# Four places in the order of a decoder layer on one core: a silu that no longer empties the list of deferred parts, the expert choice a step behind its logits, attention's reciprocal in three links of a step each, and the gate behind the next step's input

## The chip, the cores and the metric

The kernel runs on one core of one Trainium2 chip, as one program. The metric is the device time of one execution in microseconds (us), as the median of several runs. Engines are called by their short names: PE (TensorE; PEld is its loading of weights), DVE (VectorE), ACT (ScalarE), POOL (GpSimd) and SP (SyncE, here only a queue that issues DMAs).

## What is computed

One decoder layer on x of shape 8 x 512 x 512 (B x S x D), all in fp32:

```python
x = _layernorm(x + _L0_attn_ref(x, ...))           # a Mamba block
x = _layernorm(x + _L0_xattn_ref(x, ctx, ctx, mask, ...))  # cross attention, 16 heads of 32
x = _layernorm(x + _L0_ffn_ref(x, ...))            # 32 experts, 4 of them for each token

def scan_fn(h, inp):                               # in the Mamba block, over the sequence
    dA_t, dBx_t, C_t = inp
    h = dA_t * h + dBx_t
    y_t = jnp.einsum('bdn,bn->bd', h, C_t)
    return (h, y_t)
...
y = y * jax.nn.silu(z)                             # the gate
...
attn = jax.nn.softmax(scores, axis=-1)             # attention; the row sums are divided out
...
_, gtop = jax.lax.top_k(group_scores, LG)          # the choice: 4 of 8 groups of experts, then 4 experts
_, idx = jax.lax.top_k(masked, K)
...
z = jax.nn.silu(xf @ sw1) * (xf @ sw3) @ sw2       # a shared expert, for all tokens
```

The Mamba block has an inner width of 1024 and 16 states for each channel, so the recurrence runs over 8 x 1024 x 16 sequences of 512 steps. An expert takes at most 640 tokens; which place a token gets there is counted in token order.

## The kernel before

The program has three parts: `layers` (Mamba, attention, choice, shared expert), `experts` and `finish` (the last layernorm). The change lies in `layers`.

`layers` walks over 16 chunks of 256 tokens, two for each of the 8 batches; in the profile the even chunk of a pair is the first half of a batch. A chunk has 32 steps: 4 quarters q of the channels, 4 groups g of states, and 2 halves ci. A step's own work is on DVE: `steps_in` (L489, dtx times B, into the tile h), `scan` (L496, the recurrence as one scan instruction along 4 x 257 elements) and `collect` (L503, h times C). ACT computes the decays exp(A dt) of the following step ahead (`decays`, L477, four instructions); `carry` (L483, ACT) hands the state over. The sums over the states are matmuls (`products`, L513 and L523) into the PSUM tile py, issued one step later. B and C come as the tiles bc by DMAs from SP (L418), six tiles in rotation. After each 8 steps a quarter's py is complete: `gated` (L537, DVE) multiplies it into zs, and this also frees py, of which there is one. The next quarter's first product (L513) therefore stands behind the gate. `gated` runs at the beginning of the steps with k % 8 == 1.

Around this core all other work is laid in as parts: the next chunk's input (layernorm, flips, convolution, `prepare` for dt and dtx), the chunk's z (`gate_x`) and its silu at step 8, the silu of the next chunk's xs at step 24, the output projection of the chunk before (`back`, L554 and L563), and the parts of `units(b - 1)`: the whole attention, choice and shared expert of the batch before, spread by weights over the two chunks. So batch 0's Mamba has no such parts beside it, chunks 2 to 15 have those of batches 0 to 6, and the last batch's parts come after the loop, with no scan beside them.

The order on ACT, DVE and PE is the order in which this Python emits instructions (`manual_schedule`); SP's and POOL's order is a scheduler's. A part emits its PE work and returns its rest as a function, which goes into the list `left`. Each step is cut into thirds, `run(0)` ahead of the scan, `run(1)` behind the decays and `run(2)` behind `collect`; each of them calls `settle`, which runs what is due in the list. A plain function is due at the next third, one given by `wait(part)` three thirds, so one step, later. `dry()` runs all of the list at once, whatever its due time:

```python
def wait(part):
    return (clock[0] + 3 if clock else 0), part
...
def dry(force=True):
    while settle(force):
        pass
```

`finish_silu` (steps 8 and 24) calls `dry()` and then `silu` (L393 and L394: it loads ACT's table for silu, applies it, and loads the table of ln and exp again).

The parts of `units` that matter here, in their order:

- Attention, for each of 8 pairs of heads i: `maximum` (PE L831, DVE L833), `negate` (PE L840, ACT L844, DMAs L847), `weigh` (PE L857, ACT L861), `gather` (PE L873), and after its fourth piece `split` (ACT L885 copies po to raw; four DMAs, L893 and L894, bring raw to attT and to total). After each second pair, so for each of four head groups oc, `divide(oc)`: on ACT Ln and Exp(-x) of total into r (L902 and L903), on DVE a Newton step (`newton`, L906 to L908), which also multiplies attT. Since Ln and Exp are emitted in `divide` itself, Newton is due a third later.
- `output` (PE L768, DVE L925 and L926) and a layernorm, for 4 row blocks; `flip2` (PE L938, ACT L939).
- `hidden("sw1")` (PE L768, ACT L956), and after its first block `pick` (PE L590, the logits in the PSUM tile ps_l), which returns `choose` (DVE L597 to L626). From there a chain with `wait` ahead of each link: `best` four times (L633 to L642), `weights` (L648 to L657), `place` (PE L676 and L677 into the PSUM tile ps_b), `locate` (DVE L682 to L695) and 16 sends of rows to the experts' slots (L706, POOL). In chunks 3 to 13 the odd chunk's `finish_silu` at step 24 finds this chain in the list.
- `hidden("sw3")` (PE L768, DVE L954), the silu of the hidden layer, `shared` (PE L768, DVE L975 into z).

Buffers that tie these parts together: raw, nm, r, z and some others share one tag "row" with two buffers; total has one; the PSUM tag "mm" of two buffers holds ps_l, ps_b, ps_m, po and the ps_p of all dense products.

Of the kernel before, what the change touches and what calls it, by code (L numbers as in the profile page):

```python
# [8 lines left out]
F32 = mybir.dt.float32  # L9
I32 = mybir.dt.int32  # L10
U8 = mybir.dt.uint8
AF = mybir.ActivationFunctionType
ALU = mybir.AluOpType
# [4 lines left out]
P = 128  # L18
B, S, D = 8, 512, 512
DC = D // P  # L20
# [66 lines left out]
def layers(ctx, tc, a, x1d, filld, based, xbuf):  # L87
# [23 lines left out]
    nc = tc.nc  # L111
# [8 lines left out]
    p3 = ctx.enter_context(tc.tile_pool(name="l_p3", bufs=2))  # L120
# [162 lines left out]
    left, clock = [], []  # L283

    def wait(part):

        return (clock[0] + 3 if clock else 0), part
# [5 lines left out]
    def settle(force=False):  # L293

        due, later = [], []
        for x in left:
            (due if force or not clock or x[0] <= clock[0] else later).append(x)
        for _, part in due:
            rest = part()
            if rest:  # L300
                later.append(rest if isinstance(rest, tuple) else (0, rest))
        left[:] = later
        return due
# [4 lines that stand above are left out]
# [82 lines left out]
    def silu(*tiles):  # L390

        for v in tiles:
            tc.keep_in_program_order(nc.scalar.activation(v, v, AF.Silu))  # L393
        tc.keep_in_program_order(nc.scalar.preload_act_table_set(LN_EXP))  # L394
# [16 lines left out]
    def bcast(f, g):  # L411

        got = []
        for r0 in (g * NG, NST + g * NG):
            t = bcp.tile([P, NG // 2, T], F32, tag="bc", name="bc")
            for r in range(2):
                n0 = r0 + r * NG // 2
                nc.sync.dma_start(  # L418
                    t[r * HP : (r + 1) * HP], f["scr"][n0 : n0 + NG // 2, :].partition_broadcast(HP)
                )  # L420
            got.append(t.unsqueeze(1).to_broadcast([P, 2, NG // 2, T]))
        return got
# [63 lines left out]
    def steps_in(c, h, dtx, bc):  # L486

        steps = h.rearrange("p (j m) t -> p j m t", j=2)[:, :, :, 1:]
        nc.vector.tensor_tensor(  # L489
            steps, dtx[:, c % 2].unsqueeze(2).to_broadcast([P, 2, NG // 2, T]), bc[0], ALU.mult  # L490
        )
# [41 lines left out]
    def gated(q, f):  # L533

        f["xs"].pop(q)
        pair = f["zs"][:, 2 * q : 2 * q + 2, :]
        nc.vector.tensor_tensor(pair, pair, f["py"], ALU.mult)  # L537
# [46 lines left out]
    def pick(b, x2t, x2T, st):  # L584


        pl = psm.tile([P, SC, E], F32, tag="mm", name="ps_l")
        for j in range(SC):
            for dc in range(DC):
                nc.tensor.matmul(  # L590
                    pl[:, j, :], x2T[:, dc, j * P : (j + 1) * P], wg[:, dc, :], start=(dc == 0), stop=(dc == DC - 1)
                )
        return lambda: choose(b, x2t, pl, st)

    def choose(b, x2t, pl, st):
        m1 = new([1], "g_m1")
# [174 lines left out]
    def units(b):  # L771

        st = {}
# [124 lines left out]
        def divide(oc):  # L898

            attT, total = st["attT"], st["total"]  # L900
            r = p3.tile([P, D], F32, tag="row", name="r")
            nc.scalar.activation(r, total, AF.Ln)  # L902
            nc.scalar.activation(r, r, AF.Exp, scale=-1.0)  # L903

            def newton():
                nc.vector.tensor_tensor(total, total, r, ALU.mult)  # L906
                nc.vector.scalar_tensor_tensor(total, total, -2.0, r, ALU.add, ALU.mult)
                nc.vector.scalar_tensor_tensor(  # L908
                    attT[:, oc, :], attT[:, oc, :], -1.0, total, ALU.mult, ALU.mult
                )  # L910

            return newton

        def output(lt):
            if lt == 0:
# [76 lines left out]
        late = []  # L992
# [72 lines left out]
    def do(fn, *args, first=False):  # L1065

        if first:
            dry(False)
        rest = fn(*args)
        settle()  # L1070
        if rest:
            left.append(rest if isinstance(rest, tuple) else (0, rest))

    def finish_silu(*tiles):
        dry()
        silu(*tiles)

    def work(k):

        front = 6.9 if k in (2, 3) else 3.4 if 4 <= k < 8 or k in (14, 16, 19, 22, 25) else 1.0 if k in (13, 27) else 0.0  # L1080
        return 1.2 + front

    f = {"xt": x0}
# [13 lines left out]
    bc, n = bcast(f, 0), 0  # L1097
# [7 lines left out]
    for i, (b, t) in enumerate(chunks):  # L1105
        nf = {}
        after = chunks[i + 1] if i + 1 < len(chunks) else None
        if t == 0:
            side, spent = units(b - 1) if b else sources(0), 0.0

            own = [work(k) for k in range(len(steps))] * 2
            whole = sum(own) + sum(x[0] for x in side)
        for k, (q, g, ci) in enumerate(steps):
            if ci == 0:
                if (q, g) != (CC // 2 - 1, NST // NG - 1):
                    bcn = bcast(f, (g + 1) % (NST // NG))
                else:
                    bcn = bcast(nf, 0) if after else None
            h = ahead

            parts = []

            def part(fn, *args, first=False):
                parts.append((do, fn, *args, first))

            if k in (2, 3) and old:
                part(back, k - 2, *old)
            if 4 <= k < 8:
                part(gate_x, k - 4, f)
            if k == 8:  # L1130
                parts.append((finish_silu, f["zs"]))
            if k % 8 == 3:
                if q + 1 < CC // 2:
                    part(prepare, q + 1, f)
                elif after:
                    part(prepare, 0, nf)
            if after:
                if k == 10:
                    part(norm_x, nf)
                if k == 13:  # L1140
                    for j in range(DC // 2):
                        part(flip_x, j, nf)
                if k in (14, 16, 19, 22):
                    part(convolve, after[1], (14, 16, 19, 22).index(k), nf, first=(k == 14))
                if k == 24:
                    parts.append((finish_silu, *nf["xs"].values()))
                if k == 25:
                    part(x_proj, nf)
            if side and (k >= 4 or t and k < 2):
                at = t * len(steps) + k + 1  # L1150
                while side and spent + sum(own[:at]) <= whole * at / len(own):
                    w, fn, alone = side.pop(0)
                    spent += w
                    part(fn, first=alone)
            thirds = [[], [], []]
            for m, x in enumerate(parts):
                thirds[round((m + 0.5) * 3 / len(parts) - 0.5) if x[0] is do else 1].append(x)

            def run(m):
                clock[0] += 1  # L1160
                settle()
                for x in thirds[m]:
                    if x[0] is do:
                        do(*x[1:-1], first=x[-1])
                    else:
                        x[0](*x[1:])

            if k % 8 == 1:
                if k > 1:
                    gated(q - 1, f)  # L1170
                elif old:
                    gated(CC // 2 - 1, old[2])
            steps_in(2 * q + ci, h, f["ready", q][1], bc)
            if i == 0 and k == 0:
                load("Wo")
            if i == 0 and k == 2:
                biases()
            if k == 0 and old:
                twice_x(*old)
            if k == 7 and after:  # L1180
                load_x(*after, nf)
            run(0)
            scan(t, 2 * q + ci, g, das[n % 2], h)
            n += 1

            if k + 1 < len(steps) or after:
                nq, ng, ni = steps[(k + 1) % len(steps)]
                ahead = carry(t if k + 1 < len(steps) else after[1], 2 * nq + ni, ng)
                decays(2 * nq + ni, ng, (f if k + 1 < len(steps) else nf)["ready", nq][0], das[n % 2])
            run(1)  # L1190

            if products:
                products()
            products = collect(2 * q + ci, g, h, bc, f)
            run(2)
            if ci == 1:
                bc = bcn
            while i < 2 and cleared < E * (i * len(steps) + k - 6) // (2 * len(steps) - 7):
                clear(cleared)
                cleared += 1  # L1200
        while t and side:
            _, fn, alone = side.pop(0)
            do(fn, first=alone)
        old = (b, t, f)
        f = nf
# [357 lines left out]
```

## Time and profile before

| | |
|---|---|
| median of 3 runs | 5744.45 us (5741.9 to 5746.47) |
| the profiled execution | 5746.82 us, its span 5745.1 us |
| mean granted PE clock | 0.92 |
| first scan begins, last scan ends | 58.3 us, 3882.1 us |
| batch of chunks 6 and 7 | 1446 to 1937 us: PE 405.79, DVE 438.78, ACT 255.85 us busy of 491 |
| scan L496 | 512 x 2297 ns |
| L503, L489 | 512 x 1223 ns, 512 x 1218 ns |
| gate L537 | 64 x 681 ns |
| Newton L906, one of its three instructions | 32 x 692 ns |
| L902, L903 | 32 x 619 ns, 32 x 629 ns |
| table load in silu | 1283 ns, two for each silu |

A line of the groups or of a timeline names the engine, the line of the kernel, the operation and the tiles it writes and reads, then its shapes, and, where the engine stood idle before it, how long and what ended that. A line of the waits names the waiting engine, line and tile, then, after the arrow, the engine, line and tile that released it, then the total in us, the number of times, and the longest.

### The profile page before, as it was taken

The numbers are of one execution on the slowest core, as the hardware profiler recorded it, in microseconds if no ns is written. First come the engines' busy times: TensorE is split into PE (matmuls) and PEld (weight loads), VectorE is DVE, ScalarE is ACT, GpSimd is POOL, SyncE is SP. The second block draws the span as 40 slices with busy tenths as digits, with TensorE's granted clock in tenths as the row PEclk, the third lists the DMA queues.
The fourth block names the chain that finished last, engine by engine and source line by source line (L and its number), as shares of the span: only waits on it lengthen the run. The fifth ranks groups of instructions, "written<-read, shape, count | busy, mean of one in ns | idle before, by whom it ended". The sixth has DMA issues, their size and how long they took to land. (4 is left out here: it accounts for less than half of the span.)

```text
span 5745.1 us, 60272 instructions
## 1 busy us (share of the span) xinstructions
PE 4856.4 (85%) x19752; PEld 2720.4 (47%) x19752; DVE 4463.2 (78%) x5738; ACT 2507.0 (44%) x5428; POOL 485.5 (8%) x424
## 2 busy tenths in 40 slices
PE   5668878887887888788698878878899999999995
PEld 3334334433433433343343434333477777777773
DVE  6898988998898898889889888984355555555554
ACT  4454554564455455446455545632222222222223
POOL 0000001001000100100010010000111111111111
PEclk7879989998998999899899989989899999999997
DMA  6677355444534534453363444333245455444444
GB/s 190 208 220 214 100 135 156 123 117 130 168 98 117 175 112 123 138 157 111 91 202 94 133 142 142 108 95 119 78 113 123 123 123 123 123 123 123 123 122 146
DMA packets 554282, 769.83 MB, mean 134 GB/s; under 512 B 135754, under 2 KB 268394, under 8 KB 551920
## 3 DMA queue, kind: packets, MB, share of 16 engines
q1 hardware_dynamic: 517952, 677.55, 40.5%
q0 software_dynamic: 33280, 76.90, 7.2%
q10 hardware_dynamic: 2736, 11.54, 0.5%
q8 instruction: 156, 2.56, 0.2%
q14 instruction: 158, 1.29, 0.1%
HBM read 508.68 MB, written 165.05 MB: 117 GB/s over the span
## 5 line engine op out<-in xcount | busy, mean ns | idle before, releaser
L496 DVE TENSOR_TENSOR_SCAN h<-l_da,h 128x1028 f32<-128x1028 f32 x512 | 1176.0, 2297 | 67.8 <-ACT l_da L477 37.2
L477 ACT ACTIVATE l_da<-both,l_aneg 128x256 f32<-128x256 f32 x2048 | 872.6, 499 | 402.4 <-DVE h L496 396.9
L523 PE MATMUL py<-h,l_twice 128*64 128x256 f32 x4096 | 601.0, 415 | 133.8 <-DVE h L503 133.8
L503 DVE TENSOR_TENSOR h<-h,bc 128x1024 f32<-128x1024 f32 x512 | 626.1, 1223 | 12.5 <-DVE l_state L498 0.3
L489 DVE TENSOR_TENSOR h<-both,bc 128x1024 f32<-128x1024 f32 x512 | 623.4, 1218 | 6.5 <-DMA bc<-scr 6.4
L523 PEld LDWEIGHTS py<-h,l_twice 128*64 128x64 f32 x4096 | 285.8, 145 | 444.9 <-DVE h L503 180.1
L1312 PE MATMUL ps_h<-xT,w 128*128 128x320 f32 x1536 | 435.5, 433 | 0.0
L861 ACT ACTIVATE eT<-ps_t 128x1024 f32<-128x1024 f32 x256 | 260.1, 1019 | 274.2 <-PE ps_t L857 274.1
L833 DVE TENSOR_REDUCE mx<-ps_s 128x2 f32<-128x1024 f32 x256 | 310.9, 1218 | 83.9 <-PE ps_s L831 79.5
L1392 POOL DMA_INDIRECT based<-y,xe x160 | 253.2, 1582 | 1312.1 <-ACT y L1415 574.1
L831 PE MATMUL ps_s<-l_ka,l_qa 64*128 64x512 f32 x1024 | 313.2, 688 | 54.8 <-DVE mx L833 53.0
L873 PE MATMUL po<-eT,l_va 128*64 128x512 f32 x1024 | 285.2, 631 | 87.1 <-ACT eT L861 43.4
L1333 DVE TENSOR_TENSOR hT<-ps_h,p 128x320 f32<-128x320 f32 x128 | 63.0, 492 | 378.6 <-PE ps_h L1312 378.6
L1312 PEld LDWEIGHTS ps_h<-xT,w 128*128 128x128 f32 x1536 | 292.2, 190 | 118.2 <-issue 0.4
L857 PE MATMUL ps_t<-l_qa,l_ka 64*128 64x512 f32 x1024 | 279.7, 617 | 40.6 <-DVE mx L833 35.0
L1312 PE MATMUL ps_h<-t,s 128*128 128x320 f32 x1024 | 286.1, 432 | 0.0
L768 PE MATMUL ps_p<-x2T,wa 128*128 128x512 f32 x512 | 262.9, 665 | 6.6 <-ACT x2T L939 4.7
L342 PE MATMUL ps_x<-xnT,wm 128*128 128x256 f32 x1024 | 250.5, 401 | 0.3 <-ACT xnT L331 0.3
L342 PE MATMUL ps_z<-xnT,wm 128*128 128x256 f32 x1024 | 241.1, 389 | 6.3 <-DMA wm<-in_in_proj_w 6.3
L554 PE MATMUL po<-wm,zs 128*128 128x512 f32 x512 | 234.3, 611 | 10.8 <-DVE k L753 7.6
L1312 PEld LDWEIGHTS ps_h<-t,s 128*128 128x128 f32 x1024 | 194.6, 190 | 81.1
L342 PEld LDWEIGHTS ps_x<-xnT,wm 128*128 128x128 f32 x1024 | 202.7, 202 | 62.5 <-issue 23.9
(231 smaller groups left out, 7342.3 us busy)
## 6 DMA issues: line engine op xcount, KB each, us to landing
bc<-scr SPq DMA_DIRECT2D x1024, 128.0 KB
w<-in_w SPq DMA_DIRECT2D x93, 1024.0 KB
wm<-in_in_proj_w SPq DMA_DIRECT2D x128, 512.0 KB
xbuf<-zero SPq DMA_DIRECT2D x32, 1362.5 KB
xe<-xbuf SPq DMA_DIRECT2D x32, 1362.5 KB
both<-dt SPq DMA_DIRECT2D x256, 128.0 KB
both<-dtx SPq DMA_DIRECT2D x256, 128.0 KB
wm<-in_out_proj_w SPq DMA_DIRECT2D x64, 512.0 KB
```

What stands on the lines that cost most here:

```text
L342: nc.tensor.matmul(ps[:, i, :], w[:, dc, i * P : (i + 1) * P], f["xnT"][:, dc, :], start=(dc == 0), stop=(dc == DC - 1),)
L477: nc.scalar.activation(da[:, n, 1:], dt[:, c % 2, j, :], AF.Exp, scale=aneg[:, c, j, g, m : m + 1])
L489: nc.vector.tensor_tensor(steps, dtx[:, c % 2].unsqueeze(2).to_broadcast([P, 2, NG // 2, T]), bc[0], ALU.mult)
L496: nc.vector.tensor_tensor_scan(flat, da.rearrange("p n t -> p (n t)"), flat, 0.0, ALU.mult, ALU.add)
L503: nc.vector.tensor_tensor(steps, steps, bc[1], ALU.mult)
L523: nc.tensor.matmul(py[j * HP : (j + 1) * HP, c % 2, :], twice, h[:, j * 2 + m, 1:], start=False, stop=(s == (NST // NG - 1, NG // 2 - 1, 1)),)
L768: nc.tensor.matmul(ps, lhs(dc), rhs(dc), start=(dc == 0), stop=(dc == DC - 1))
L831: nc.tensor.matmul(ps[:, j, :], qa[r, lt * P : (lt + 1) * P], ka[r, :], start=True, stop=True)
L833: return lambda: nc.vector.tensor_reduce(mx[:, lt, :].unsqueeze(2), ps, AX.X, ALU.max) and None
L857: nc.tensor.matmul(ps[:, j, :], ka[r, kc * P : (kc + 1) * P], qa[r, :], start=True, stop=True)
L873: nc.tensor.matmul(po[j * 2 * HD : (j + 1) * 2 * HD, :], va[:, kc, i, j * HD : (j + 2) * HD], eT[:, j, :], start=(kc == 0), stop=(kc == SC ...
L1312: nc.tensor.matmul(ps, w[:, n, r * P : (r + 1) * P], x[:, n, :], start=not more and n == 0, stop=n == 1, skip_group_check=more,)
```

## The change

Nothing is computed in another way; four things are emitted at other places.

1. `pick` returns `wait(choose)`: the choice is due a step after its logits were issued, not at the next third.
2. In `divide`, for the head groups 0 to 2, Ln and Exp are emitted a step later, and Newton a step after them. The last group has no waits.
3. `finish_silu` empties the list only if `clock` is empty, that is outside the loop. In the loop it goes straight to the silu.
4. The gate is emitted behind `steps_in` of its step, not ahead of it.

```diff
--- before.py
+++ after.py
@@ -590,7 +590,7 @@
                 nc.tensor.matmul(
                     pl[:, j, :], x2T[:, dc, j * P : (j + 1) * P], wg[:, dc, :], start=(dc == 0), stop=(dc == DC - 1)
                 )
-        return lambda: choose(b, x2t, pl, st)
+        return wait(lambda: choose(b, x2t, pl, st))
 
     def choose(b, x2t, pl, st):
         m1 = new([1], "g_m1")
@@ -898,18 +898,24 @@
         def divide(oc):
 
             attT, total = st["attT"], st["total"]
-            r = p3.tile([P, D], F32, tag="row", name="r")
-            nc.scalar.activation(r, total, AF.Ln)
-            nc.scalar.activation(r, r, AF.Exp, scale=-1.0)
-
-            def newton():
-                nc.vector.tensor_tensor(total, total, r, ALU.mult)
-                nc.vector.scalar_tensor_tensor(total, total, -2.0, r, ALU.add, ALU.mult)
-                nc.vector.scalar_tensor_tensor(
-                    attT[:, oc, :], attT[:, oc, :], -1.0, total, ALU.mult, ALU.mult
-                )
-
-            return newton
+
+            late = wait if oc < DC - 1 else lambda part: part
+
+            def inverse():
+                r = p3.tile([P, D], F32, tag="row", name="r")
+                nc.scalar.activation(r, total, AF.Ln)
+                nc.scalar.activation(r, r, AF.Exp, scale=-1.0)
+
+                def newton():
+                    nc.vector.tensor_tensor(total, total, r, ALU.mult)
+                    nc.vector.scalar_tensor_tensor(total, total, -2.0, r, ALU.add, ALU.mult)
+                    nc.vector.scalar_tensor_tensor(
+                        attT[:, oc, :], attT[:, oc, :], -1.0, total, ALU.mult, ALU.mult
+                    )
+
+                return late(newton)
+
+            return late(inverse)
 
         def output(lt):
             if lt == 0:
@@ -1072,7 +1078,8 @@
             left.append(rest if isinstance(rest, tuple) else (0, rest))
 
     def finish_silu(*tiles):
-        dry()
+        if not clock:
+            dry()
         silu(*tiles)
 
     def work(k):
@@ -1165,12 +1172,12 @@
                     else:
                         x[0](*x[1:])
 
+            steps_in(2 * q + ci, h, f["ready", q][1], bc)
             if k % 8 == 1:
                 if k > 1:
                     gated(q - 1, f)
                 elif old:
                     gated(CC // 2 - 1, old[2])
-            steps_in(2 * q + ci, h, f["ready", q][1], bc)
             if i == 0 and k == 0:
                 load("Wo")
             if i == 0 and k == 2:
```

## The prediction

> **What bounds the kernel now.** I read the page's busy shares and slices first, then the waits by engine, then, stretch by stretch, the timeline of one batch (chunks 6 and 7, 1446 to 1937 us), whose gaps return in every batch from chunk 2 on.
>
> ```profile
> PE 4856.4 (85%) x19752; PEld 2720.4 (47%) x19752; DVE 4463.2 (78%) x5738; ACT 2507.0 (44%) x5428; POOL 485.5 (8%) x424
> PE   5668878887887888788698878878899999999995
> DVE  6898988998898898889889888984355555555554
> ```
>
> PE leads over the span, but only through the last third (the experts). In the scan loop (first scan 58.3, last ends 3882.1 us) DVE leads:
>
> ```profile
> 1446.00:1937.00 491.00, 405.79 (x1684) 194.32 (x1684) 438.78 (x498) 255.85 (x556) 29.93 (x29) 0.92 0.46 132
> 1868.00:1886.00 18.00, 1.00 (x8) 0.57 (x5) 16.58 (x36) 6.57 (x10) 0.00 (x0) 0.64 0.09 30
> ```
>
> The third number is PE's busy time, the sixth (438.78) DVE's: of 491 us a batch DVE idles 52 and PE 85. PE's idleness is in a few stretches, of which 1868 to 1886 is the emptiest. Elsewhere PE runs without a gap for 25 to 55 us and sets the pace. So the loop is DVE's, with places where DVE stands behind a PE that is solid; 7 batches have the side work.
>
> What DVE waits for:
>
> ```profile
> DVE total L906 <- ACT r L903: 79.7, 16, 12.1
> DVE g_m L597 <- PE ps_l L590: 68.6, 8, 12.4
> DVE h L496 <- ACT l_da L477: 37.2, 21, 9.4
> DVE zs L537 <- ACT zs L393: 25.0, 8, 4.6
> DVE hT L954 <- PE ps_p L768: 18.1, 9, 2.7
> DVE zs L537 <- PE py L523: 8.9, 11, 1.6
> PE ps_b L676 <- DVE g_any L655: 104.2, 7, 17.0
> ```
>
> Columns: total us, times, longest. L906, L597 and L537 are the heads of the parts that the diff moves; the last row is PE waiting for the choice.
>
> [...] L597 stands in DVE's order ahead of L503 and L489 of the next step, and both follow it at 1859.75 and 1860.88 though their scan and their bc had been there during the 8.32 us wait. [...] Here each L393 and L394 load is 1283 ns, 40 times each; the change leaves their number and their places on ACT as they are, so they enter no sum. [...]
>
> **The change part by part.** Removed and added: nothing; instructions per engine stay equal, only places in the orders move. After the loop the orders on PE, ACT and DVE are unchanged, and the experts (4134 us to the end) are the same. So all of it is gaps of the loop.
>
> *The choice a step later.* Before, it stands right behind a scan:
>
> ```profile
> 1843.83 2.29 DVE L496 TENSOR_TENSOR_SCAN h<-l_da,h 128x1028 f32<-128x1028 f32 x1
> 1854.44 0.29 DVE L597 TENSOR_REDUCE g_m<-ps_l 128x4 f32<-128x128 f32 x1 [8.32 <-PE ps_l L590]
> ...
> 1859.75 1.22 DVE L503 TENSOR_TENSOR h<-h,bc 128x1024 f32<-128x1024 f32 x1
> 1860.88 1.22 DVE L489 TENSOR_TENSOR h<-both,bc 128x1024 f32<-128x1024 f32 x1
> 1862.13 2.30 DVE L496 TENSOR_TENSOR_SCAN h<-l_da,h 128x1028 f32<-128x1028 f32 x1
> ```
>
> In the changed order it stands behind L503 and L489, still ahead of the next scan. ps_l doesn't come earlier: PE works without a gap from 1845.17 (shared expert 5.74, ps_l 3.65). So of 8.32 us only L503 + L489 less an overlap of issue, 1.22 + 1.22 - 0.09 = 2.35, is filled; 6.0 stays. 7 x 2.35 = 16.5 us. From both sides: 0 if PE's ps_l slips as much, 7 x 8.3 = 58 if more work came before it, which the order excludes.
>
> *The silu that drains the list.* In odd chunks, at step 24, the deferred choice chain (two rounds of best, weights, placing) was forced out at once. PE's ps_b for it stood ahead of shared-expert matmuls, so PE stood 17.00 us for L655, and then DVE waited for PE: L682 0.73, the gate's py 0.9, L954 1.87, and 0.46 at the scan, 3.5 to 3.96 in chunks 3 to 13. In the changed order the rounds lie in steps 23 to 26, weights in 27, placing in 29, and ps_b comes 46 PE instructions later. The DVE work (best 1.8 each, weights 2.3, placing 5.2 us) is only moved. New: placing holds one of two "mm" PSUM buffers until L684, and the shared z product on PE queues behind that, 0.15 to 0.3 us by L682 + L684 (0.21 x 4 + 0.28 less overlap); ACT's hT, the sends on POOL (16 x 1.3 us) and DVE's later steps are behind it. Net 3.0 x 6 = 18 us; bounds 0 (PE, filled again, is only late elsewhere) and 6 x 4 = 24. At step 8 the order doesn't change, so the 2.91 us wait for silu(zs) in even chunks isn't touched by this edit.
>
> *The reciprocal in three links.* For three of the four head groups Ln and Exp go a step later on ACT, and the Newton step (3 x 0.69 us) another on DVE. Groups 0 and 1 have no gap at L906: 0. The fourth is written without waits and keeps its order. Group 2 has, at step 12 of odd chunks, the first line below:
>
> ```profile
> 1770.37 0.69 DVE L906 TENSOR_TENSOR total<-total,r 128x512 f32<-128x512 f32 x1 [2.74 <-ACT r L903]
> ...
> 1788.36 1.22 DVE L503 TENSOR_TENSOR h<-h,bc 128x1024 f32<-128x1024 f32 x1
> 1789.60 1.31 SPq L418 DMA_DIRECT2D bc<-scr  x2
> 1791.01 0.55 SPq L893 DMA_DIRECT2D attT<-raw  x1
> 1796.49 0.69 DVE L906 TENSOR_TENSOR total<-total,r 128x512 f32<-128x512 f32 x1 [6.92 <-ACT r L903]
> ```
>
> The 2.74 us goes. Whether it is given back is asked of group 3, 20 us on, where DVE waits 6.92 + 1.03 for that group's reciprocal. Its row sums leave PE and ACT by 1785.7 (raw, L885), but SP's queue holds the DMA behind a bc load that waits for DVE's L503, done at 1789.58. So up to 3.9 us of DVE's lead shortens that chain too, and 2.74 fits. I take 2.4 of it (part may end at PE, solid until 1788.3), 6 times, and 1.6 for chunk 15, where the same wait is 2.6 us: 16 us. Bounds: 0, and 7 x 2.7 plus the 6.4 us of chunk 15's last group, 25.
> The added waits: the total<-raw DMAs of the next group (total has one buffer) now wait for L907/L908 of the group before, on SP, with bc loads behind them. For group 3 they would issue from 1778.8 on, and Newton, 2.07 us behind the scan that begins about 1773.7, ends at 1778.1: covered, by 0.7 us; if not, a bc load 3 steps ahead of its use is late by less than that lead. r holds one of two "row" buffers longer, so in group 0 ACT's nm (L844) waits some 5 us for the Newton step with four decays (1.70 us) behind it; replayed with the durations above, these are ready 3 us before their scan. 0; without that cover about 2 to 5 us a batch, and this goes into the range.
>
> *The gate behind steps_in.* At step 1 of each 8, DVE does L489 (1.22) before the gate (0.68). Where the gate waits, for zs (25.0 us, 8 times) or py (8.9, 11 times), up to 1.2 us of L489 goes into the wait: at most 8 x 1.2 + 7.6 = 17, some 10 inside the periodic stretches. Against it, PE gets its next py buffer 1.22 us later, 64 times. Where PE is solid behind a gate (1450.4 to 1504.4, after it stood 5.21 us for that gate) the delay comes out at DVE's next wait for PE: 8 x 1.2 lost. I take -0.4 a batch, 3 us lost; bounds a gain of 17 and, as the last rival, a loss of 78.
>
> **The sum.** 16.5 + 18 + 16 - 3 = 47.5 us. The profiled execution took 5746.82 us (span 5745.1 and 1.7 around it): 5746.8 - 47.5 = 5699.3. It lies 2.4 above the median of 5744.45, so the forecast is 5697, -0.83%. As each term has its own bounds, this case's own range is 5680 to 5720.
>
> **The rivals.**
> *The waits vanish whole.* 58 (choice) + 25 + 8 (gate) + 24 (list) + 25 (reciprocal) = 140: 5605. For it: each named wait is on DVE, the fullest engine. Against: ps_l's end is PE's, the gate's zs is ACT's, and neither moves. A half of what is between, 5655 to 5680 (say 5670), can come if PE, no longer stopped 17 us a batch, brings the next chunk's products earlier and so shortens waits that I left alone (L563, L753, dtx).
> *The waits only move.* The step-24 gap and the 2.74 us come back in the 6.9 us at group 3 and the 6 us at ps_l, which end by PE; only the choice's fill stays, or half of it: 5744 - 8 to 16 = 5732. For it: PE has 25 to 55 us stretches without a gap; against: SP's order behind L503, above, and PE's 17 us, which it gets back just ahead of its next solid stretch.
> *It doesn't do what it says.* At step 8, and in the drain after the loop, order and so time stay; were the list emptied elsewhere just as hard, 0 of the 18: 5715, inside the range.
> *Slower: PE led by the gate.* PE's L513 already waited for the gate:
>
> ```profile
> PE py L513 <- DVE zs L537: 63.6, 21, 6.1
> ```
>
> Each gate hands PE its buffer 1.22 us late, 64 times, 78 us if every one reaches DVE: 5697 + 78 = 5775; with 3 already counted and three quarters of them, 5753. It decides from 39 of 64 (47.5/1.22) on: as many would have to be in stretches where PE has under 1.2 us of slack before DVE needs it. Against: PE's 85 idle us a batch, and only 21 of 64 gates were waited for. I put it at 5765.
>
> **How the numbers follow.** Likeliest (5680 to 5720, at 5697): 0.50. Between the sum and the whole (5640 to 5680): 0.13; the whole, below 5640: 0.03. Waits only move, 5720 to 5744: 0.22, about half of it within 0.2% (11.5 us, about what a measurement of this kernel can tell from no change). Slower, 5744 and up: 0.12, of it 0.03 under 11.5 us. So faster 0.77, same 0.14, slower 0.09. The range 5662 to 5743 leaves out the 0.12 above and about 0.07 below.
>
> **What would show it.** Right: L597's wait falls from 8.3 to about 6 with L503 and L489 ahead of it; PE's wait for g_any goes from 17 us to under 1 each; L906's 2.7 us gaps are gone while 6 to 7 us stay at group 3; DVE busy is unchanged and chunks 3 to 13 are shorter by 6 to 8 us, even ones by less than 1. Wrong: chunks as long as before with a longer wait at L597 or at group 3 (waits move); L513's wait for the gate growing beyond 100 us with even chunks longer (the slower rival); SP's bc loads late, seen as waits of L489 for bc.

## The result, and the profile after

The changed kernel takes 5703.33 us (5701.63 to 5706.09), against 5744.47 before in the same comparison: a ratio of 0.9929, 95% interval 0.9912 to 0.9946, 41 us less. The forecast was 5697, with a range from 5662 to 5743. The profiled execution took 5701.63 us, its span 5699.5.

The page's busy time and PE's slices, of the changed kernel:

```profile
PE 4877.2 (86%) x19752; PEld 2717.2 (48%) x19752; DVE 4454.8 (78%) x5738; ACT 2506.3 (44%) x5428; POOL 496.4 (9%) x424
PE   5668888897887888789788888878899999999995
```

The counts of instructions are those of before, and the work after the loop is too: from the start of the last scan to the end of the span both traces have 1865.3 us. All the difference lies in the loop.

DVE's waits for the parts that the prediction named, changed kernel (us in total, times, longest):

```profile
DVE mx L833 <- PE ps_s L831: 101.3, 56, 3.3
DVE total L910 <- ACT r L907: 68.5, 11, 12.1
DVE o L563 <- PE po L554: 53.7, 30, 13.3
DVE h L496 <- ACT l_da L477: 46.7, 29, 9.7
DVE g_m L597 <- PE ps_l L590: 38.5, 8, 12.4
DVE zs L537 <- ACT zs L393: 17.7, 8, 5.5
```

L597 fell by 30.1 us, the wait for the reciprocal (L906 before, now L910) by 11.2 and by two more waits of 6.4 and 2.6 that were put down to DMAs, that for zs by 7.3, and the three that the prediction set behind the drained list (L954, L682, and L537 for py) from 31.3 to 8.8. But the wait at L833, which the change doesn't touch, is up from 79.5 to 101.3, that at L563 from 36.7 to 53.7, and that for the decays (L496) from 37.2 to 46.7: 48 us came back elsewhere. PE's long wait for the choice is gone (104.2 us before), and its wait for the gate has grown, as the changed kernel's waits of PE show:

```profile
PE py L513 <- DVE zs L537: 75.0, 27, 7.2
...
PE ps_b L676 <- DVE g_any L655: 2.0, 1, 2.0
```

The choice now stands behind the next step's L503 and L489, and 3.42 us of its 8.32 us wait are left:

```profile
1831.12 1.22 DVE L503 TENSOR_TENSOR h<-h,bc 128x1024 f32<-128x1024 f32 x1
1832.27 1.22 DVE L489 TENSOR_TENSOR h<-both,bc 128x1024 f32<-128x1024 f32 x1
1836.91 0.29 DVE L597 TENSOR_REDUCE g_m<-ps_l 128x4 f32<-128x128 f32 x1 [3.42 <-PE ps_l L590]
```

That is 4.9 us less, where moving 2.35 us of work ahead of the wait could take off 2.35. The rest is on PE. The eight matmuls ahead of ps_l, before:

```profile
1845.17 5.74 PE L768 MATMUL ps_p<-x2T,wa 128*128 128x512 f32 x8 [0.68 <-ACT x2T L939]
```

and after:

```profile
1829.68 3.70 PE L768 MATMUL ps_p<-x2T,wa 128*128 128x512 f32 x8 [0.68 <-ACT x2T L945]
```

They are the same eight matmuls behind the same wait, 2.04 us apart: before, four of them and a part of the fifth ran at half clock. (PE had stood still for 8.09 us ahead of the first flip and for 3.57 us ahead of the second, and its granted clock was 0.50 from 1829 to 1849 us; in the changed kernel it was 1.00 from 1829.7 to 1836 us.) This made me look at how long a batch takes. The first scans of chunks 6, 7 and 8, before:

```profile
1445.89 2.30 DVE L496 TENSOR_TENSOR_SCAN h<-l_da,h 128x1028 f32<-128x1028 f32 x1
1682.09 2.29 DVE L496 TENSOR_TENSOR_SCAN h<-l_da,h 128x1028 f32<-128x1028 f32 x1
1937.63 2.30 DVE L496 TENSOR_TENSOR_SCAN h<-l_da,h 128x1028 f32<-128x1028 f32 x1
```

and after:

```profile
1428.33 2.30 DVE L496 TENSOR_TENSOR_SCAN h<-l_da,h 128x1028 f32<-128x1028 f32 x1
1669.20 2.29 DVE L496 TENSOR_TENSOR_SCAN h<-l_da,h 128x1028 f32<-128x1028 f32 x1
1913.10 2.30 DVE L496 TENSOR_TENSOR_SCAN h<-l_da,h 128x1028 f32<-128x1028 f32 x1
```

The odd chunk 7 became 11.6 us shorter (255.54 to 243.90), but the even chunk 6 4.7 us longer (236.20 to 240.87). So it is in all batches from chunk 4 to chunk 14: odd chunks 11.3 to 11.6 us shorter, even ones 4.6 to 4.7 longer. In chunk 6 the loss stands in waits for PE: 3.27 us in place of 0.82 at L563, and 8.0 in place of 4.7 at L833.

As a mean of these five batches a batch takes 491.51 us before and 484.69 after. In both traces PE's granted clock, 1.00 or 0.50, switches on a grid with a period of 3.4133 us, as the last section shows; one such period is called a window from here on. 491.51 / 3.4133 = 144.00, and 484.69 / 3.4133 = 142.00. The change took exactly two of these windows off each of five batches (34.1 us), 10.6 off the batch of chunks 2 and 3, 0.7 off the last two chunks and 0.2 off what lies ahead of chunk 2: 45.6 us of span. The batch of chunks 2 and 3, the first with side work, isn't a whole number of windows (500.05 and 489.42 us); in both kernels the whole numbers begin with chunk 4.

### The profile page after: what moved, and what is told of

The parts are those of the page before. It is cut to its first block, busy times and chain, and to the rows that moved or that the text cites. A ratio compares the mean times of both kernels' runs of the same rounds, so it can differ in the third digit from the quotient of the medians.

```text
span 5699.5 us, 60267 instructions
## 1 busy us (share of the span) xinstructions
PE 4877.2 (86%) x19752; PEld 2717.2 (48%) x19752; DVE 4454.8 (78%) x5738; ACT 2506.3 (44%) x5428; POOL 496.4 (9%) x424
## 3 DMA queue, kind: packets, MB, share of 16 engines
q14 instruction: 157, 1.29, 0.1%
## 5 line engine op out<-in xcount | busy, mean ns | idle before, releaser
L496 DVE TENSOR_TENSOR_SCAN h<-l_da,h 128x1028 f32<-128x1028 f32 x512 | 1175.3, 2295 | 69.1 <-ACT l_da L477 46.7
L523 PE MATMUL py<-h,l_twice 128*64 128x256 f32 x4096 | 603.7, 418 | 159.7 <-DVE h L503 159.6
L503 DVE TENSOR_TENSOR h<-h,bc 128x1024 f32<-128x1024 f32 x512 | 626.1, 1223 | 13.1 <-DVE l_state L498 0.3
L489 DVE TENSOR_TENSOR h<-both,bc 128x1024 f32<-128x1024 f32 x512 | 623.4, 1217 | 6.7 <-DMA bc<-scr 6.7
L523 PEld LDWEIGHTS py<-h,l_twice 128*64 128x64 f32 x4096 | 288.1, 147 | 482.4 <-DVE h L503 213.8
L833 DVE TENSOR_REDUCE mx<-ps_s 128x2 f32<-128x1024 f32 x256 | 310.9, 1218 | 105.4 <-PE ps_s L831 101.3
L831 PE MATMUL ps_s<-l_ka,l_qa 64*128 64x512 f32 x1024 | 325.6, 715 | 66.8 <-DVE mx L833 65.7
L873 PE MATMUL po<-eT,l_va 128*64 128x512 f32 x1024 | 304.8, 671 | 88.0 <-ACT eT L861 44.2
L861 ACT ACTIVATE eT<-ps_t 128x1024 f32<-128x1024 f32 x256 | 259.9, 1018 | 270.8 <-PE ps_t L857 270.7
L768 PE MATMUL ps_p<-x2T,wa 128*128 128x512 f32 x512 | 251.5, 638 | 27.5 <-DVE hT L960 22.8
L554 PE MATMUL po<-wm,zs 128*128 128x512 f32 x512 | 241.4, 625 | 10.2 <-DVE k L753 6.5
L706 POOL DMA_INDIRECT xbuf<-x2t,dest x128 | 175.0, 1367 | 808.5 <-DVE z L975 301.6
```

Of the source, the lines that this page charges most:

```text
L489: nc.vector.tensor_tensor(steps, dtx[:, c % 2].unsqueeze(2).to_broadcast([P, 2, NG // 2, T]), bc[0], ALU.mult)
L496: nc.vector.tensor_tensor_scan(flat, da.rearrange("p n t -> p (n t)"), flat, 0.0, ALU.mult, ALU.add)
L503: nc.vector.tensor_tensor(steps, steps, bc[1], ALU.mult)
L523: nc.tensor.matmul(py[j * HP : (j + 1) * HP, c % 2, :], twice, h[:, j * 2 + m, 1:], start=False, stop=(s == (NST // NG - 1, NG // 2 - 1, 1)),)
L831: nc.tensor.matmul(ps[:, j, :], qa[r, lt * P : (lt + 1) * P], ka[r, :], start=True, stop=True)
L833: return lambda: nc.vector.tensor_reduce(mx[:, lt, :].unsqueeze(2), ps, AX.X, ALU.max) and None
```

## The experiments

Two theories went into them beside my sum: that waits only move, and that a batch lasts whole windows. The times, medians; "batch" is the distance between the first scans of even chunks, from chunk 4 to chunk 14, five values:

| kernel | us | ratio to before (95%) | batch, us | windows |
|---|---|---|---|---|
| before | 5743 to 5746 | | 491.2 to 491.7 | 144 |
| changed | 5703.3 | 0.9929 (0.9912 to 0.9946) | 484.6 to 484.8 | 142 |
| choice alone | 5742.7 | 0.9994 (0.9986 to 1.0002) | 491.4 to 491.5, once 488.3 | 144, once 143 |
| list alone | 5725.2 | 0.9965 (0.9953 to 0.9977) | 487.9 to 488.3 | 143 |
| reciprocal alone | 5739.6 | 0.9990 (0.9983 to 0.9996) | 491.4 to 491.7 | 144 |
| gate alone | 5759.6 | 1.0026 (1.0016 to 1.0035) | 494.9 to 495.1, once 498.1 | 145, once 146 |
| all but the gate | 5692.8 | 0.9909 (0.9893 to 0.9926) | 484.6 to 484.7 | 142 |
| changed, DVE +0.69 us | 5695.6 | 0.9918 (0.9901 to 0.9934) | 484.3 to 484.9, once 481.3 | 142, once 141 |
| changed, DVE +2.08 us | 5697.9 | 0.9920 (0.9904 to 0.9937) | 484.5 to 484.9 | 142 |
| changed, fillers of 6.3 us | 5713.3 | 0.9941 (0.9925 to 0.9958) | 488.0 to 488.2 | 143 |
| changed, fillers of 2.8 and 3.7 us | 5670.7 | 0.9873 (0.9857 to 0.9890) | 481.1 to 481.4, once 478.1 | 141, once 140 |
| no gate, choice two steps late | 5741.7 | 0.9996 (0.9987 to 1.0005) | 491.1 to 494.9 | not whole; between odd chunks 144, once 145 |
| no gate, fillers at the flips | 5682.6 | 0.9896 (0.9879 to 0.9912) | 481.2 to 481.5, once 484.4 | 141, once 142 |
| changed, both fillers | 5673.0 | 0.9875 (0.9858 to 0.9891) | 480.6 to 481.9 | near 141; between odd chunks 141 |

**The choice alone.** The kernel before, with

```diff
-        return lambda: choose(b, x2t, pl, st)
+        return wait(lambda: choose(b, x2t, pl, st))
```

> The kernel before with the wait for the choice alone. By my working (terms that add): 2.35 us off each batch, 16.5 us in all, so about 5728, and a batch (from the first scan of one even chunk to that of the next) of 489.2 us. A second theory, drawn from the two traces: the batch takes 491.52 us before and 484.70 after, 144 and 142 times 3.4133 us[...]; a batch then changes only by whole windows, so 491.52 (no gain, 5744) or 488.11 (5724 to 5727), and nothing between. That waits only move: 491.5.

5742.7, no change that can be told. Its waits of DVE:

```profile
DVE mx L833 <- PE ps_s L831: 87.0, 59, 3.1
DVE g_m L597 <- PE ps_l L590: 52.1, 8, 12.3
DVE o L563 <- PE po L554: 46.8, 30, 13.8
```

L597's wait fell from some 8.3 to 6.1 us in five of the seven batches, as I had worked out. It came back in the following even chunk, where L563 waits for po by 2.3 instead of 0.8 us and L833 twice by 1.1: the batch is where it was, at 144 windows. One batch jumped to 143. "The waits only move" is right for this edit alone.

**The list alone.**

```diff
     def finish_silu(*tiles):
-        dry()
+        if not clock:
+            dry()
```

> The kernel before with finish_silu that leaves the list alone in the loop, nothing else. By my working 3.0 us off each of 6 batches, 18 us, about 5726, a batch of 488.5 us; PE's wait for g_any of 17 us gone. By whole windows: 488.11 (5724 to 5727), or 491.52 (5744), as PE also loses the stretch at half clock behind its 17 us of idleness. That waits only move: 5740 or more.

5725.2: 20.8 us off, one window in each batch. It is the only edit that takes a window off every batch by itself, and the time is near what I gave it (18 us).

**The reciprocal alone.** The `divide` of the diff, in the kernel before.

> The kernel before with the reciprocal in three links alone. By my working 2.4 us off a batch and 1.6 in chunk 15, 16 us, about 5728, a batch of 489.1 us, with the 2.74 us gap at step 12 of odd chunks gone and 6 to 7 us left at the last head group. By whole windows 491.52 or 488.11. That waits only move: L906's gap goes into the last group's or L597's wait, 5740 to 5745.

5739.6: 6.4 us, not 16. The 2.74 us gap is gone, but the scan of step 14 now waits 1.4 us for its decays, and the batch stays at 144 windows. Its trace is 9.5 us shorter, of which 5.3 lie in the last two chunks, which no further chunk follows, and the rest ahead of chunk 4 and behind the last scan.

**The gate alone.**

```diff
+            steps_in(2 * q + ci, h, f["ready", q][1], bc)
             if k % 8 == 1:
                 ...
-            steps_in(2 * q + ci, h, f["ready", q][1], bc)
```

> The kernel before with the gate behind the next step's input alone. By my working 0.4 us more a batch, 3 us, about 5747, a batch of 491.9 us: even chunks begin with a longer wait for po (L563) and get it back at the wait for zs at step 8. By whole windows 491.52 (5744) or 494.93 (5762 to 5765). The rival of a PE led by the gate: 5752 to 5775.

5759.6: 13.6 us slower. PE at the start of chunk 8 in this kernel:

```profile
1947.67 1.12 PE L513 MATMUL py<-xs,l_ident 128*64 128x256 f32 x4 [6.34 <-DVE zs L537]
1948.55 1.95 PE L523 MATMUL py<-h,l_twice 128*64 128x256 f32 x8
1950.43 8.43 PE L554 MATMUL po<-wm,zs 128*128 128x512 f32 x16
```

PE stands still longer for the later gate (before 5.21 us, in chunk 6), and the L554 matmuls behind it begin at half clock (before, in chunk 6, 16 took 7.22 us, at a granted clock of 1.00). Behind the first scan of chunk 6 the half clock lasts one window longer than before (three in place of two: the granted clock is 0.53 as a mean from 1443.9 to 1454 us; before it is 0.50 from 1446.6 to 1453.3 us and 1.00 behind that). DVE's wait at L563 goes up from 0.8 to 3.3 us in even chunks, a batch by one window, once by two.

The four alone add up to 3.3 + 20.8 + 6.4 - 13.6 = 17 us, where together they bring 41. So the terms don't add.

**All but the gate.** The changed kernel with the gate back ahead of `steps_in`.

> The changed kernel with the gate back ahead of the next step's input. By terms that add (the gate alone cost 13.6 us): 5703 - 13.6 = 5690, a batch of 482.7 us. By whole windows of 3.4133 us: 141 or 140 of them, so a batch of 481.28 or 477.87 and 5683 or 5663, or 142 as now and no gain. By my first working, which gave the gate 3 us: 5700.

5692.8, some 10 us better than the changed kernel. The two intervals, taken beside different runs of before, overlap. In the traces the batches are the same 142 windows; of the 5.4 us between the two, 5.1 are in the last two chunks, 467.1 us with the gate and 462.0 without. Inside a batch only the place of the waits differs: L597 waits 6.2 to 6.3 us without the gate and 3.4 with it, L563 1.0 without and 3.3 with it. A sum of terms had 482.7 us a batch; in fact the gate costs a window alone, and none in the same batches beside the other three.

**More work for DVE.** At step 26 of odd chunks, once or three times:

```diff
+            if t and i > 2 and k == 26:
+                for _ in range(1):
+                    nc.vector.tensor_tensor(bo, bo, bo, ALU.max)
```

> The changed kernel with one DVE instruction more in step 26 of each odd chunk from chunk 3 on (the maximum of a constant with itself, 0.69 us, no effect on the result), where DVE is the fullest engine and waits for nothing. If DVE's work and waits simply add: 0.69 us a batch, 485.38 us, and 5708. By whole windows: a batch of 484.69 as now (5703), or of 488.11 (5723), nothing between.

> The same with three such instructions, 2.08 us. If work and waits add: a batch of 486.77 us, 5718. By whole windows: 484.69 (5703 to 5706) or 488.11 (5723), nothing between.

5695.6 and 5697.9: no slower than the changed kernel's 5703.3 (why 5 to 8 us less is open: with three doses no batch is shorter), though the fullest engine of the loop has up to 2.08 us more to do in each batch. With three doses every batch is still 142 windows, not the 486.77 us of a sum. Its DVE waits show who paid:

```profile
DVE mx L833 <- PE ps_s L831: 90.3, 66, 3.1
...
DVE o L563 <- PE po L554: 47.6, 30, 12.3
```

The waits at L833 and L563 are 11.0 and 6.1 us shorter than in the changed kernel. Here added work was taken out of the wait for PE, as work taken away was put into it.

**PE kept busy at the chunk boundary.** In the changed kernel PE stands still twice there, and works at half clock (chunk 8; the granted clock is 0.50 from 1911 to 1924 us):

```profile
1911.32 1.98 PE L523 MATMUL py<-h,l_twice 128*64 128x256 f32 x8 [4.06 <-DVE h L503]
1918.74 1.12 PE L513 MATMUL py<-xs,l_ident 128*64 128x256 f32 x4 [5.45 <-DVE zs L537]
1919.62 1.95 PE L523 MATMUL py<-h,l_twice 128*64 128x256 f32 x8
1921.50 8.30 PE L554 MATMUL po<-wm,zs 128*128 128x512 f32 x16
```

DVE waits for the end of this:

```profile
1936.64 0.75 DVE L563 SCALAR_TENSOR_TENSOR o<-po,l_rs,o 128x512 f32<-128x512 f32 x1 [3.23 <-PE po L554]
```

The experiment adds matmuls of constants behind the products at steps 31 and 0:

```diff
             if products:
                 products()
+            if i > 2 and (t, k) in ((1, 31), (0, 0)):
+                ps = pss.tile([P, 2, S], F32, tag="sc", name="ps_warm")
+                for _ in range(7):
+                    nc.tensor.matmul(ps[:, 0, :], ident, bo, start=True, stop=True)
```

> The changed kernel with seven matmuls more (128 x 128 by 512, of constants, read by nobody) on PE behind the products at step 31 of odd and at step 0 of even chunks, where PE stands still for 4.1 and 5.5 us and then runs at half clock until 10.4 us into the even chunk. If the half clock behind those idle stretches is what holds DVE at po (L563, 3.27 us), that wait falls below 1 us, the batch gets shorter by 1 to 3.4 us, and the time to 5683 to 5697. If the clock has nothing to do with it, PE's 3 us more work twice a batch leave the time where it is, or make it longer by up to 6 us a batch (5703 to 5740).

5713.3, a miss by two side effects. Seven matmuls take 6.28 us, more than I had reckoned, and SP's scheduler put a part of L554's weights behind three more bc loads, so that PE waited for it, as its waits show:

```profile
PE po L554 <- DMA wm<-in_out_proj_w: 20.6, 7, 3.5
```

With three and four matmuls (`range(3 if k else 4)`) the weights keep their place:

> The changed kernel with three matmuls more behind the products at step 31 of odd chunks and four at step 0 of even ones (128 x 128 by 512, of constants, read by nobody; 0.9 us each by the run before, where seven were 6.28 us and SP's load of wm came behind more bc loads; here wm keeps its place). PE's 4.1 and 5.5 us of idleness shrink to some 1.4 and 1.9. If the half clock behind them holds DVE at po, the first 16 L554 matmuls take 7.13 in place of 8.34 us, L563 waits under 2.2 in place of 3.27 us, and a batch is 1 us or a whole window shorter: 5683 to 5697. If the clock doesn't matter there: 484.69 us or up to 3 more, 5703 or above.

5670.7, 33 us better than the changed kernel, by matmuls that compute nothing. PE in its trace, at the same boundary:

```profile
1894.04 2.84 PE L1204 MATMUL ps_warm<-l_bo,l_ident 128*128 128x512 f32 x6
1898.17 1.09 PE L523 MATMUL py<-h,l_twice 128*64 128x256 f32 x8 [1.29 <-DVE h L503]
1899.19 3.70 PE L1204 MATMUL ps_warm<-l_bo,l_ident 128*128 128x512 f32 x8
1905.60 0.65 PE L513 MATMUL py<-xs,l_ident 128*64 128x256 f32 x4 [2.71 <-DVE zs L537]
1906.05 1.06 PE L523 MATMUL py<-h,l_twice 128*64 128x256 f32 x8
1907.04 7.13 PE L554 MATMUL po<-wm,zs 128*128 128x512 f32 x16
```

The idle stretches are 1.29 and 2.71 us, L523 takes 1.06 in place of 1.95 us and L554 7.13 in place of 8.30, the durations of full clock (in the changed kernel eight matmuls of L523 take 1.03 us at 1445.48 us, where the granted clock is 1.00). L563 waits 0.74 or 0.75 us in five of six even chunks (1.74 in chunk 8). A batch is one window shorter, once two.

**The choice two steps late.** All but the gate, and

```diff
-        return wait(lambda: choose(b, x2t, pl, st))
+        return wait(lambda: wait(lambda: choose(b, x2t, pl, st)))
```

> The kernel with the gate in its old place, and the choice two steps behind its logits in place of one. A step more is at least 4.8 us of DVE work, so of the 6.2 us at L597 at most 1.4 stay. If terms add: 4.8 us a batch, 479.9 us, 5692.8 - 34 = 5659. By whole windows: 481.28 or 477.87, so 5672 or 5652. If waits only move (PE's later half-clock stretch and the last head group then end as late as before): 484.69, 5693.

5741.7, 49 us worse than one step. The wait for ps_l is gone, but the choice's exponential on ACT (L600) moved behind other work there:

```profile
1860.93 0.59 ACT L962 COPY hT<-ps_p 128x512 f32<-128x512 f32 x1 [5.05 <-PE ps_p L768]
...
1865.38 0.59 ACT L362 COPY xp<-ps_x 128x512 f32<-128x512 f32 x1 [2.17 <-PE ps_x L342]
...
1867.06 0.30 ACT L600 ACTIVATE g_sc<-g_sc 128x128 f32<-128x128 f32 x1
```

and DVE, in the middle of the choice, stands for it:

```profile
1867.39 0.29 DVE L601 TENSOR_REDUCE g_m<-g_sc 128x4 f32<-128x128 f32 x1 [7.06 <-ACT g_sc L600]
```

Measured between the first scans of odd chunks its batches are whole as well: 491.5 to 491.6 us, once 494.9. None of my three theories had the wait for ACT. At one step's distance the wait for L600 is 0.38 us.

**PE kept busy ahead of the flips.** All but the gate, with fillers in `output(0)`, `flip2(0)` and `flip2(1)` (six, seven and two):

> The kernel with the gate in its old place, and matmuls without a reader where PE stands still ahead of the attention's output (six, of 8.3 us idleness), ahead of the first flip (seven, of 6.4 to 8.1 us) and of the second (two, of 3.6 us). If the half clock there, up to 1833 us in the trace of that kernel, sets ps_l's end: L768 and L590 at full clock, L597's wait of 6.2 us down by 2 to 3.4 us, a batch of 481.28 us or off the whole windows, 5670 to 5685. If not: 484.69 us or more, 5693 or above.

5682.6, 10 us better than without, and one window less in four of five batches. In these four L597 waits 3.4 to 3.6 us; in the fifth, which stayed at 142 windows, 6.3 as before.

**Both.**

> The changed kernel with both sets of matmuls without a reader: at the chunk boundary (three and four, as in the run that gave 5670.7) and ahead of the attention's output and the first two flips (six, seven and two, which alone took 10 us off the kernel with the gate in its old place). If each half-clock stretch costs by itself: 5660 to 5663, a batch of 478 to 480 us. By whole windows: 477.87 or 474.45 a batch, 5652 or 5634; or 481.28 as before, 5671, if the first set had taken the only stretch that counted. If no half-clock stretch on DVE's path is left, the batch leaves the multiples of 3.4133 us.

5673.0: no better than the chunk boundary's fillers alone. Now the half clock set in at the third flip, behind the last filler, and the eight matmuls ahead of ps_l are as slow as in the kernel before (5.74 us):

```profile
1818.80 5.86 PE L768 MATMUL ps_p<-x2T,wa 128*128 128x512 f32 x8 [0.68 <-ACT x2T L955]
```

L597 waits 4 to 6 us. PE had stood still for 2.1, 2.3 and 1.0 us within 9 us, with two flips and two fillers between, and the granted clock is 0.50 from 1812.95 to 1823.19 us.

## Why the prediction was right, and where it wasn't

*The sum.* Right in size: 47.5 us forecast, 41 in the medians, 45.6 in the spans. But it took the four edits as independent terms, and they are not. This is the step that failed. Each alone, they bring 3, 21, 6 and -14 us. From chunk 4 on the batches of both kernels lasted whole numbers of windows (144 and 142 of 3.4133 us), so an edit counted when it carried the batch over the next boundary, and what was left of it went into a wait for PE. By my terms a batch was to lose 2.35 + 3.0 + 2.4 - 0.4 = 7.35 us; it lost 6.82, since that is two windows. That these lie so close together was luck. How a batch came by it was not as forecast either: I had odd chunks shorter by 6 to 8 us and even ones by less than 1, and the odd ones are shorter by 11.3 to 11.6 and the even ones longer by 4.6 to 4.7. Longer even chunks were a part of my sign for the rival of a PE led by the gate; its other part, over 100 us at L513, did not come (75.0).

*What was passed over.* I left PE's clock out. I took the 5.74 us that PE worked ahead of ps_l as fixed, and so the end of ps_l; the changed kernel ran the same eight matmuls in 3.70 us, at a granted clock of 1.00. A smaller reading: in the prediction's row of the batch DVE's 438.78 is the fifth number.

*The choice.* The fill of 2.35 us is right, as the run with it alone shows (8.3 to 6.1 us). As time it was nothing alone. The other 2.55 us off L597 in the changed kernel are PE's: 2.04 of them in eight matmuls, by their clock. They bought no time: all but the gate has the same 142 windows with 6.3 us at L597.

*The list.* The cause is right: PE's 17 us stretches are gone, and in the run with this edit alone the waits that I named fell from 3.75 to 1.03 us in chunk 7 (a wait of 1.64 us for py came up earlier in that chunk). The size, 20.8 us alone for 18, is near because my 3.0 us a batch are near one window of 3.41. The added wait of the shared expert's z for a PSUM buffer, 0.15 to 0.3 us, doesn't show in the trace.

*The reciprocal.* The gap went and group 3 kept its 6.4 to 6.9 us, both as forecast. What I gave the late Ln and Exp was wrong by the next in line: with DVE no longer held at step 12, ACT, which has exponentials (L861) and the layernorm's L331 ahead of its decays, is late for step 14 by 1.38 us in chunk 7. In the run with this edit alone group 3's reciprocal did come 1.4 us earlier, counted from the first scan of chunk 6 (349.2 in place of 350.6 us). But full clock came back ahead of the choice at 403.6 in place of 403.4, the choice began at 408.3 in place of 408.5 with a wait of 8.71 in place of 8.32 us, and the batch stayed at 491.5. So what I let pass of the chain behind SP's queue, 2.4 of 2.74 us, ended at PE.

*The gate.* Mis-sized: -0.4 us a batch in my sum, a whole window (3.4 us) in the run with it alone. I saw PE's delay at the start of even chunks and the 1.13 us that come back at zs (2.91 to 1.78 us, as forecast). I did not see that with 1.1 us more of idleness (6.34 us in place of 5.21) PE would stay at half clock for a window longer. The last rival had its place right and its mechanism wrong: as far as the trace shows, what cost was PE's clock behind the gate of even chunks (three windows at 0.50 in place of two), not 64 late buffers. No run with fillers in this kernel tested it.

*The rivals.* "The waits vanish whole" is out. "The waits only move" holds for the choice and for most of the reciprocal, each alone.

*Open.* No run has the list with only one of choice and reciprocal, so which of these two brings the second window, or whether it takes both, is not shown. Which half-clock stretch holds the batch in the kernel before was not tried; the fillers show it only for the chunk boundary of the changed kernel and, less sharply, for the flips. The traces point to the stretch ahead of the choice: in the kernel before, the choice begins 5.0 to 5.1 us after full clock came back in four of five batches, with the reciprocal alone 4.7 to 4.8 in all five, and in the changed kernel, where the half clock ends a window earlier, 8.5 to 8.6. That a batch keeps its whole number by itself is shown by the kernels of the table. How the clock brings this about was not shown. It is my argument that, since each return to full clock in the traces of the kernel before and of the changed one lies on the grid, what waits for the matmuls around it is tied to the grid too.

## What to carry to other kernels

Before adding up small gaps in a loop, look whether PE works at half clock anywhere on the path (matmuls of one line with two durations, here eight of L523 in 1.06 or 1.95 us; a granted clock of 0.50), and whether the period is a multiple of one time (here of 3.4133 us). If so, gains can come in steps, and single edits can show nothing or all (here a window in each batch for the list, none in most for the choice). Where PE idles just ahead of matmuls that another engine waits for, a few matmuls of constants in the idle stretch can be worth more than taking waits away (seven at the chunk boundary took 33 us off); see that they end before the awaited work comes, and that they don't move a DMA in a scheduler's order (with fourteen there PE waited 20.6 us in all for wm).

## What the hardware showed that was not expected

In these traces PE's granted clock changes on a fixed grid. One return to full clock in the changed kernel, at 1923.89 us (the third number from the end of a row is the granted clock in that stretch):

```profile
1920.00:1923.88 3.88, 3.88 (x11) 1.70 (x8) 3.71 (x5) 1.79 (x5) 3.27 (x3) 0.50 1.03 400
1923.91:1930.00 6.09, 6.09 (x16) 2.48 (x16) 5.92 (x5) 1.71 (x4) 0.49 (x1) 1.00 0.93 330
```

Others are at 1439.20, 1787.36 and 1828.32 us: 348.16, 40.96 and 95.57 us apart, which is 102, 12 and 28 times 3.4133. In the trace's record of the clock every switch, to half and back, lies on one grid of 3.4133 us to within 0.003 us, in the kernel before (179 switches) and in the changed one (197).

The loop fell into step with this grid. In the kernel before, the first scans of chunks 0 and 2 begin 0.95 and 1.11 us behind a point of the grid, and those of all even chunks from 4 to 14 2.6 to 3.0 us behind one; in the changed kernel 1.34 and 1.47, then 2.7 to 2.9. Eleven of the fourteen kernels have batches of whole windows to within 0.4 us, from 140 to 146, and a twelfth to within 0.42; the other two have them to within 0.1 us when the batch is measured between odd chunks.

More full clock was not less time by itself. The changed kernel's mean granted clock is 0.922; with the fillers at the chunk boundary (three and four matmuls) it is 0.933 and with both sets 0.94, yet both sets are no faster (5673.0 and 5670.7 us): here the share of half clock counted less than where it lay.
